# Both scans of a tile couple first, then both products with C, on VectorE

## The chip, the cores and the metric

The kernel runs on one core of one Trainium2 chip. The metric is the device time of one execution in microseconds; a comparison is made between runs of the two kernels on the same chip. In the text, DVE is VectorE, ACT is ScalarE, POOL is GpSimd, PE is TensorE and SP is SyncE, whose queue issues all the transfers spoken of here.

## The reference

The reference is a small network of four layers on an image batch of 4 x 96 x 64 x 64 in float32. Layer 0 is a selective scan (a state-space block) over four directions of each image; layer 1 is an inverted-residual convolution; layer 2 a Fourier mixing layer with a quantised feed-forward; layer 3 linear attention with another quantised feed-forward. The change is in layer 0. Cut to its core, with 192 channels `d`, 16 states `n` and 4 directions `k`, each of 4096 positions:

```python
def step(hst, inp):                       # one position
    ut, dt_, bt, ct = inp
    dA = jnp.exp(dt_[..., None] * A[None])
    hst = hst * dA + (dt_ * ut)[..., None] * bt[:, :, None, :]
    y = jnp.einsum('bkdn,bkn->bkd', hst, ct)
    return (hst, y)
_, ys = jax.lax.scan(step, h0, (u_t, d_t, B_t, C_t))
```

So for each channel and state there is a first-order recurrence along the positions, and the output sums, over the 16 states, the state times `C`.

## The kernel before

**Tiles.** One step of the scan stage handles one image, one direction and one chunk of 512 positions; there are 4 x 4 x 8 = 128 steps. The 192 x 16 recurrences of a step lie in 12 units. A unit, here called a couple, has two tiles of 128 partitions x 512 positions, e = 0 and e = 1. The functions that make a couple are nested in `scans`:

- `inputs` (L1213): POOL multiplies `rep_g` (delta times u) by B into the buffer `db`, both tiles in one instruction (L1215). There are 3 `db` buffers.
- `decays` (L1217): ACT computes exp(delta times A) into two of the four PSUM banks with the tag `da`, one instruction for each e (L1225). Just before each of the two it calls `keep` for the couple two places back.
- `states` (L1227): DVE runs the recurrence as a tensor-tensor scan over `da` and `db` (L1234). Of the 12 couples of a step, 5 (`POOL_C`) have the scan's result written into the buffer `hc` in SBUF, and POOL multiplies it by C afterwards, both tiles in one instruction (`product`, L1253). In the other 7 the scan writes in place, into its `da` bank, and DVE itself multiplies by C into `hc` (L1238). There are 5 `hc` buffers.
- `keep` (L1240): the last column of the scanned tile is copied to `state`, where the next chunk of the same direction starts. ACT does it for each e (L1248) where DVE made the product, POOL for both at once (L1250) where POOL makes it.
- `sums` (L1263): PE adds up the 16 states of two couples with the constant `stack` matrix, into the bank `y` (L1274), first for the later couple and there for e = 1. After the last couple of a pass, ACT copies `y` to `yt` (L1285).

An exponential may overwrite a `da` bank only when the couple that used it has been scanned and, where DVE makes the product, multiplied and kept.

**Order.** The scan stage is recorded under a manual schedule: every engine executes its instructions in the order in which Python emits them. The loop over slots emits, for the couple `units[slot]`:

```python
decays(units[slot + 1], units[slot - 1] if slot > 0 else None)
...
product(units[slot - 1])
...
inputs(units[slot + 2])
...
states(x)
for group in due.get(slot, ()):
    sums(group)
```

`product` is called only for a couple whose product POOL makes. After these calls, the loop calls `advance` as long as the slot has room: it emits single instructions of the other layers' work, here called side work, by a planner with estimated costs (`WORK`, `RATE`, `SHARE`). So the side work of PE, ACT and DVE stands between one couple and the next, at places that don't depend on the measured time. The loads of `rep_d`, `rep_g` and `rep_BC`, 512 KB each, are issued by SP at fixed couples of a step (`LOADS`).

**Waits.** Instructions of different engines, and dependent instructions of one engine, are held together by semaphores. `keep` on ACT waits for DVE's product of the same e, the second exponential of a slot for whatever used its bank.

Of the kernel before, what the change touches and what calls it, by code (L numbers as in the profile page):

```python
# [94 lines left out]
def hybrid_kernel(ctx: ExitStack, tc: tile.TileContext, a: dict):  # L95
# [10 lines left out]
    pool = lambda name, bufs=1, **kw: ctx.enter_context(tc.tile_pool(name=name, bufs=bufs, **kw))  # L106
# [75 lines left out]
    def pair(tag):  # L182
        return sp.tile([128, 2, CH], F32, name=tag, tag=tag, bufs=SCAN[tag])
# [973 lines left out]
    def scans(stages):  # L1157
# [69 lines left out]
        def states(x):  # L1227
            step, u = x["step"], x["u"]
            order = slice(None, None, -1) if step["k"] >= 2 else slice(None)
            x["hc"] = pair("hc")  # L1230
            x["h"] = [x["hc"][:, e] for e in (0, 1)] if x["pool"] else x["da"]
            for e in (0, 1):
                start = 0.0 if step["n"] == 0 else steps[x["number"] - 1]["last"][:, 2 * u + e : 2 * u + e + 1]
                nc.vector.tensor_tensor_scan(  # L1234
                    x["h"][e][:, order], x["da"][e][:, order], x["db"][:, e, order], start, ALU.mult, ALU.add
                )
                if not x["pool"]:
                    x["made"] = nc.vector.tensor_mul(x["hc"][:, e], x["h"][e], x["step"]["BC"][x["j"]][:, 1])  # L1238

        def keep(x, e):  # L1240
# [61 lines left out]
        for slot in range(len(units) + 6):  # L1302
            clock[0] = slot
            x = units[slot] if slot < len(units) else None
# [23 lines left out]
            if x is not None:  # L1328
                states(x)
# [252 lines left out]
```

## Time and profile before

| What | us |
|---|---|
| median of 3 runs | 6582.01 |
| lowest and highest run | 6569.84, 6595.57 |
| profiled execution, first to last instruction | 6603.1 |
| of that, from the first scan (79.2) to the end of the last (6129.9) | 6050.7 |
| after it | 473.2 |
| scans in place, 1792, busy and mean | 2278.6, 1279 ns (with a state), 1219 ns (without) |
| scans into `hc`, 1280, busy and mean | 1557.3, 1266 ns (with a state), 1203 ns (without) |
| DVE's products with C, 1792, busy and mean | 1239.3, 692 ns |
| POOL's `db`, 1536, busy and mean | 3601.2, 2365 ns |
| POOL's products with C, 640, busy and mean | 1512.0, 2363 ns |
| ACT's exponentials, 3072, busy and mean | 2067.3, 690 ns |

The profiled execution's own time is shown only as this span, from its first instruction to its last. It is one execution, and the runs are others; the counts are of instructions. Busy time is what the profiler records of an instruction from its start to its end; neighbours on one engine may overlap a little, so starts tell more than durations. The profile also tells how long an engine sat idle ahead of an instruction and which instruction of another engine ended that wait.

### The profile page before, as it was taken

What the parts mean: (1) busy time and instruction counts of PE and PEld (TensorE: products, weight loads), DVE (VectorE), ACT (ScalarE), POOL (GpSimd) and SP (SyncE); (2) the same over time, 40 slices, a digit from 0 to 9 for tenths busy, and PEclk for the clock granted to TensorE, in tenths of its full rate; (3) what the DMA queues carried; (4) which work ended last, traced back from release to release, by engine and by line L of the source; (5) the groups of instructions that cost most, each with busy time, mean ns of one, the idle gap of its engine ahead of it and who ended that gap; (6) DMA issues with size and microseconds to landing.
All of it is one profiled execution on the core that took longest, in us unless ns stands there. A gap on an engine that the chain in (4) does not pass through costs nothing. (4 is left out here: it accounts for less than half of the span.)

```text
span 6603.1 us, 84466 instructions
## 1 busy us (share of the span) xinstructions
PE 4803.7 (73%) x27804; PEld 1767.2 (27%) x27804; DVE 5616.6 (85%) x5947; ACT 4265.1 (65%) x8152; POOL 5183.5 (79%) x2743
## 2 busy tenths in 40 slices
PE   7633857757987776775688877667887776758997
PEld 2100212111224521221122254211223621112383
DVE  5979999999999889999899998988999889898113
ACT  5743777765665677787466657766665677756356
POOL 4757878789998889987899988988999788898100
PEclk9755978868998877886799878878988877979998
DMA  5644565676544544466764455465644544655131
GB/s 186 200 153 136 188 202 188 198 234 226 178 155 158 178 151 144 161 196 195 239 211 159 148 175 172 140 225 176 188 155 154 176 153 165 198 191 170 34 97 40
DMA packets 438826, 1121.42 MB, mean 170 GB/s; under 512 B 73002, under 2 KB 74768, under 8 KB 437140
## 3 DMA queue, kind: packets, MB, share of 16 engines
q1 hardware_dynamic: 438388, 1116.02, 51.6%
q8 instruction: 221, 3.62, 0.2%
q14 instruction: 217, 1.78, 0.1%
HBM read 881.28 MB, written 239.01 MB: 170 GB/s over the span
## 5 line engine op out<-in xcount | busy, mean ns | idle before, releaser
L1215 POOL TENSOR_TENSOR db<-rep_g,rep_BC 128x1024 f32<-128x1024 f32 x1536 | 3601.2, 2365 | 474.3 <-DVE ps_da L1234 357.7
L1225 ACT ACTIVATE ps_da<-rep_d,aneg 128x512 f32<-128x512 f32 x3072 | 2067.3, 690 | 557.2 <-DVE hc L1234 423.1
L1234 DVE TENSOR_TENSOR_SCAN ps_da<-ps_da,state,db 128x512 f32<-128x512 f32 x1568 | 2005.6, 1279 | 209.8 <-ACT state L1248 162.0
L1253 POOL TENSOR_TENSOR hc<-hc,rep_BC 128x1024 f32<-128x1024 f32 x640 | 1512.0, 2363 | 116.0 <-DVE hc L1234 59.4
L1274 PE MATMUL ps_y<-hc,cst 128*32 128x512 f32 x6144 | 1024.8, 745 | 660.9 <-POOL hc L1253 413.4
L1234 DVE TENSOR_TENSOR_SCAN hc<-ps_da,state,db 128x512 f32<-128x512 f32 x1120 | 1371.3, 1266 | 82.2 <-ACT ps_da L1225 54.8
L1238 DVE TENSOR_TENSOR hc<-ps_da,rep_BC 128x512 f32<-128x512 f32 x1792 | 1239.3, 692 | 109.8 <-PE ps_y L1274 1.5
L1248 ACT COPY state<-ps_da 128x1 f32<-128x1 f32 x1568 | 247.8, 158 | 525.4 <-DVE hc L1238 521.5
L1274 PEld LDWEIGHTS ps_y<-hc,cst 128*32 128x32 f32 x6144 | 145.9, 118 | 1298.1 <-POOL hc L1253 641.4
L1250 POOL COPY state<-hc 128x2 f32<-128x2 f32 x560 | 106.8, 191 | 353.1 <-DVE hc L1234 337.1
L805 PE MATMUL ps_mm<-h,wd 128*32 128x512 f32 x3192 | 366.9, 595 | 8.7 <-ACT r L154 8.7
L543 PE MATMUL ps_mm<-xp,taps 128*128 128x512 f32 x576 | 299.5, 663 | 52.2 <-ACT ua L545 21.5
L1234 DVE TENSOR_TENSOR_SCAN ps_da<-ps_da,db 128x512 f32<-128x512 f32 x224 | 273.0, 1219 | 41.0 <-ACT state L1248 27.8
L782 PE MATMUL ps_mm<-wd,w 128*32 128x512 f32 x2128 | 272.0, 621 | 37.7 <-DMA wd<-x 22.3
L1285 ACT COPY yt<-ps_y 128x512 f32<-128x512 f32 x256 | 149.1, 582 | 162.8 <-PE ps_y L1274 161.2
L594 PE MATMUL ps_mm<-xd,dtw 128*128 128x512 f32 x256 | 171.0, 760 | 101.3 <-ACT z L616 56.2
L955 PE MATMUL ps_mm<-wa,xp 128*64 128x96 f32 x1728 | 139.7, 324 | 88.8 <-DVE d L959 71.5
L864 PE MATMUL ps_mm<-r,cst 128*128 128x512 f32 x208 | 146.6, 794 | 70.7 <-ACT r L861 17.8
L1234 DVE TENSOR_TENSOR_SCAN hc<-ps_da,db 128x512 f32<-128x512 f32 x160 | 186.0, 1203 | 3.0 <-ACT ps_da L1225 2.9
L786 ACT ACTIVATE h<-ps_mm 128x512 f32<-128x512 f32 x266 | 152.4, 596 | 48.2 <-PE ps_mm L782 46.6
L543 PEld LDWEIGHTS ps_mm<-xp,taps 128*128 128x128 f32 x576 | 116.7, 210 | 230.4 <-issue 163.2
L805 PEld LDWEIGHTS ps_mm<-h,wd 128*32 128x32 f32 x3192 | 105.5, 109 | 251.9 <-issue 210.1
(405 smaller groups left out, 6856.2 us busy)
## 6 DMA issues: line engine op xcount, KB each, us to landing
rep_BC<-bc SPq DMA_DIRECT2D x512, 512.0 KB
rep_g<-du SPq DMA_DIRECT2D x384, 512.0 KB
rep_d<-delta SPq DMA_DIRECT2D x384, 512.0 KB
y<-yt SPq DMA_DIRECT2D x512, 128.0 KB
du<-g SPq DMA_DIRECT2D x128, 256.0 KB
delta<-z SPq DMA_DIRECT2D x128, 256.0 KB
tab<-in_etab SPq DMA_DIRECT2D x128, 256.0 KB
ypart<-y SPq DMA_DIRECT2D x72, 256.0 KB
```

The lines of the kernel that those rows point to most:

```text
L543: mm(p, lhsT=taps[:, t, 0:128], rhs=window(t, c + e), start=t == 0, stop=t == 8)
L594: mm(p, lhsT=dtw[:, o + 2 * part, 0:128], rhs=xd, start=True, stop=True)
L782: mm(p[32 * n : 32 * n + 32], lhsT=w1[:, 32 * g : 32 * g + 32], rhs=xin[:, n : n + 15 : 2, 1 : W + 1], start=True, stop=True)
L786: act(h[:, :, 1 : W + 1], split(p), AF.Relu)
L805: mm(p[32 * n : 32 * n + 32], lhsT=held["wd"][:, groups[i], o, dx, :], rhs=here[i][:, :, dx : dx + W], start=dx == 0, stop=dx == 2)
L1215: nc.gpsimd.tensor_mul(x["db"], x["step"]["g"][x["i"]], both(x["step"]["BC"][x["j"]][:, 0]))
L1225: act(x["da"][e], x["step"]["d"][x["i"]][:, e], AF.Exp, scale=aneg[:, av : av + 1])
L1234: nc.vector.tensor_tensor_scan(x["h"][e][:, order], x["da"][e][:, order], x["db"][:, e, order], start, ALU.mult, ALU.add)
L1238: x["made"] = nc.vector.tensor_mul(x["hc"][:, e], x["h"][e], x["step"]["BC"][x["j"]][:, 1])
L1248: nc.scalar.copy(to[:, e : e + 1], x["h"][e][:, end : end + 1])
L1253: x["made"] = nc.gpsimd.tensor_mul(x["hc"], x["hc"], both(x["step"]["BC"][x["j"]][:, 1]))
L1274: done = mm(y[32 * q : 32 * q + 32], lhsT=const("stack"), rhs=x["hc"][:, e], start=first or (x["pass"] == 0 and x["j"] == 0), stop=last or ...
```

## The change

In `states`, the product with C leaves the loop over e that issues the scans and gets a loop of its own behind it. In the 7 couples of a step whose product DVE makes, DVE's order becomes scan 0, scan 1, product 0, product 1, where it was scan 0, product 0, scan 1, product 1. The other 5 couples keep their order. The product's line becomes L1239, and the lines behind it move by one.

```diff
             for e in (0, 1):
                 start = 0.0 if step["n"] == 0 else steps[x["number"] - 1]["last"][:, 2 * u + e : 2 * u + e + 1]
                 nc.vector.tensor_tensor_scan(
                     x["h"][e][:, order], x["da"][e][:, order], x["db"][:, e, order], start, ALU.mult, ALU.add
                 )
-                if not x["pool"]:
+            if not x["pool"]:
+                for e in (0, 1):
                     x["made"] = nc.vector.tensor_mul(x["hc"][:, e], x["h"][e], x["step"]["BC"][x["j"]][:, 1])
```

## The prediction

> **What bounds the kernel now.** I read the busy shares first, then the slices, then three stretches, then single VectorE (DVE) instructions, then the waits.
>
> The page's busy shares and two of its rows of slices:
>
> ```profile
> PE 4803.7 (73%) x27804; PEld 1767.2 (27%) x27804; DVE 5616.6 (85%) x5947; ACT 4265.1 (65%) x8152; POOL 5183.5 (79%) x2743
> ...
> DVE  5979999999999889999899998988999889898113
> ...
> POOL 4757878789998889987899988988999788898100
> ```
>
> DVE leads, but GpSimd (POOL) is close, and both stop after slice 37: the scan stage runs from 79 to 6130 us, and a tail of 473 us follows it that the change doesn't touch. The scan stage has 128 steps of 12 couples; cutting it at every 24th scan shows three kinds of step. One of each, from the view by stretches (length, then each engine's busy time and instruction count):
>
> ```profile
> 1276.03:1329.75 53.72, 35.83 (x94) 6.98 (x87) 52.63 (x58) 43.03 (x85) 41.57 (x23) 0.82 0.61 196
> 3575.69:3616.28 40.59, 32.09 (x174) 10.24 (x166) 39.14 (x45) 25.25 (x52) 40.19 (x23) 0.92 0.50 165
> 4022.60:4069.22 46.62, 39.31 (x326) 25.73 (x325) 38.60 (x39) 33.30 (x59) 41.37 (x24) 0.82 0.61 195
> ```
>
> The columns are PE, weight loads, DVE, ACT, POOL. The first step is DVE's alone (52.6 of 53.7). In the second POOL is busy for 40.2 of 40.6 and DVE for 39.1: both are full. In the third nobody is full; DVE waits there for ACT. I sorted all 128: **DVE-full**, 30 steps, 1475 us, DVE 47.7 us busy a step; **both full**, 36 steps, 1486 us, mean 41.3 us with POOL 39.8 and DVE 40.1; **waiting**, 62 steps, 3090 us, with 418 us of DVE waits over 0.1 us.
>
> Where DVE's time goes inside a couple, from the timeline of DVE alone (start, duration; "x2" is two in a row):
>
> ```profile
> 1276.03 1.28 DVE L1234 TENSOR_TENSOR_SCAN ps_da<-ps_da,state,db 128x512 f32<-128x512 f32 x1
> 1277.35 0.69 DVE L1238 TENSOR_TENSOR hc<-ps_da,rep_BC 128x512 f32<-128x512 f32 x1
> 1277.95 1.28 DVE L1234 TENSOR_TENSOR_SCAN ps_da<-ps_da,state,db 128x512 f32<-128x512 f32 x1
> 1279.27 0.69 DVE L1238 TENSOR_TENSOR hc<-ps_da,rep_BC 128x512 f32<-128x512 f32 x1
> 1279.88 2.45 DVE L1234 TENSOR_TENSOR_SCAN hc<-ps_da,state,db 128x512 f32<-128x512 f32 x2
> 1282.24 0.67 DVE L609 SCALAR_TENSOR_TENSOR ps_mm<-ps_mm,z 128x512 f32<-128x512 f32 x1
> ```
>
> Read starts, not durations. A product that reads the scan just before it starts 1.32 us after that scan: the scan's whole 1.28 plus 0.04. An instruction that doesn't depend on its predecessor starts before that one is recorded as ended: scan 2 comes 0.60 after product 1, whose record is 0.69 long, and the two scans of the last couple, whose product POOL makes, take 2.36 together, so 1.18 each. Over the trace the medians are: first scan to product 1358 ns, second scan to product 1316, product to anything 608, scan to independent scan 1190, scan to anything else independent 1175. So each scan-to-product step pays some 0.14 us for the dependence.
>
> Who waits for whom, in three lines of the waits:
>
> ```profile
> DVE ps_da L1234 <- ACT state L1248: 189.9, 97, 7.5
> POOL db L1215 <- DVE ps_da L1234: 357.7, 167, 42.6
> ACT state L1248 <- DVE hc L1238: 521.5, 405, 45.7
> ```
>
> DVE waits for ACT in 97 places, POOL hardly ever holds DVE up, and ACT and POOL wait for DVE more than it waits for them.
>
> [...] and POOL's `db` product has a median of 2362 ns over 1536 of them, so I expect no effect from the new order on POOL's durations.
>
> **The change, part by part.** Nothing is added or removed. In the 896 couples whose product DVE makes (1792 products, L1238), scan 2 moves ahead of product 1. The built programs show POOL's and SP's instructions in the same order with the same waits, so no transfer moves; PE's and ACT's order is the same too, and only some waits shift to a neighbouring instruction.
>
> *DVE.* Before: 1.32 + 0.61 + 1.32 + 0.61 = 3.86 us for a couple (3.85 in the lines above, 3.89 from the medians). After: scan 1 to scan 2 1.19, scan 2 to product 1 1.18, then 0.61 + 0.61 = 3.59. Product 2 needs scan 2, whose end at 1.19 + 1.28 + 0.04 = 2.51 lies before its turn at 2.98. Two in-place scans in a row don't occur before; the lower bound is 1.18 (scans into `hc`), the upper 1.32 (a full dependence). I take 1.19[...]. The gain is 0.27 to 0.31, I take 0.29: 896 x 0.29 = 260 us of DVE time. That is the ceiling.
>
> *ACT.* `keep` e = 0 and the exponential behind it wait for product 1, which now ends 3.06 us after the couple's start instead of 2.01. Behind them in ACT's queue stand `keep` e = 1 and the second exponential, waiting for product 2 in either order, and then the side work, so nothing else is held up. Product 2 ends at 3.67 instead of 3.94. ACT still has the first exponential (0.69) to do then, so the second starts 0.35 after product 2, not 0.23: 3.67 + 0.35 = 4.02 against 4.17, 0.15 earlier. What the first exponential fills is scanned at least one couple (2.36) later. Cost: nothing, while that cover holds.
>
> *POOL and PE.* Scan 2 frees `db` at 2.47 instead of 3.21, so POOL may start sooner; PE's sums wait for product 2, 0.27 sooner. No cost.
>
> *What of the 260 lies on the path.* I followed the trace from the last scan to the first, at each instruction to whichever came last, the engine's own predecessor or a wait. 921 of the 1792 products are on that chain: 336 in DVE-full steps, 280 in both-full ones, 305 in waiting ones. At 0.145 each these are 49, 41 and 44 us. In DVE-full steps POOL (39.5 busy of 49 us) leaves room: I take 47. In both-full steps POOL is next: its intervals (2.32 for each of 12 `db`, 2.58 for each of 5 products with its copy) make 40.7 of the mean 41.3: I take 15. In waiting steps a DVE that comes sooner partly waits longer for ACT, which sits behind matmuls: I take 33. Sum 95 us. The span of 6603.1 us would become 6508, a factor of 0.9856. The profile shows no time around that span; it lay 21 us above the median of the runs, and I apply the factor to the median: 6582 x 0.9856 = 6487 us.
>
> **Rivals.**
>
> *Full conversion (faster still).* If ACT's waits are themselves set by DVE (it waited 521.5 us for products), waiting steps gain the full 7 x 0.29 = 2.0 us. 92 steps outside "both full" x 2.0 = 184, plus 22: about 205 us, 6378 us. Against it: the chain holds only 305 products in those 62 steps, and it runs mostly through PE there.
>
> *No overlap, or hidden (no change).* If in-place scans in PSUM follow each other only at 1.28 to 1.32, the couple takes 3.78 to 3.86; with half on the chain, 0 to 40 us. Or POOL, PE and ACT together take up all but the DVE-full steps, and half of those: 25 us. About 6557 us. For it: three engines near full in the second stretch.
>
> *The second exponential comes late (slower).* Scan 2 is now due 1.19 after scan 1, not 1.93. In the changed program 239 DVE couples take for scan 2 a bank that scan 2 of the couple just before, a POOL one, has just left. There the exponential can start 2.49 after that couple's start and ends at 3.18, visible at about 3.25; scan 2 is due at 2.36 + 1.19 = 3.55. The slack falls from 1.0 to 0.3 us. If ACT is late by x there, DVE loses x - 0.3 in each: the gain of 95 is gone from x = 0.7, and slower by 0.5% from 0.84. With one 0.69 exponential and a 0.58 copy ahead, x = 1.27 costs 232 us: net 137 slower, 6719 us. Against it: ACT is busy for 65% and mostly waits for DVE.
>
> **How the numbers follow.** Forecast 0.60, full conversion 0.17, no change 0.16, slower 0.07. The likeliest gives 6487 us. Its own range is a gain of 55 to 140. For 8 in 10 it reaches up into full conversion (185 us: 6397) and down to a gain of 15 us (6567). A measurement of this kernel can tell about 0.5%, 33 us, from no change: faster needs a gain over 33, which the forecast and full conversion hold nearly whole; slower by as much takes the third rival.
>
> **What would show it.** In the changed profile, two scans in a row and then two products should start 1.19, 1.18 and 0.61 apart, and the couple take 3.58 to 3.62; the mean idle time ahead of the products (L1239 then) should fall from 61 ns to about nothing. DVE-full steps should lose about 2 us each, both-full ones stay at 40.5 to 41, POOL's share of the scan stage rise from 85% to 87%. DVE's waits for ACT should grow from 293 us by some 100. Scans 1.28 or more apart prove the no-change rival; DVE waits for ACT that grow by more than 260 us, ahead of second scans, prove the slower one; a shift of ACT's side work that leaves the waits as they are proves full conversion.

## The result and the profile after

| What | before | after |
|---|---|---|
| median of the runs, us | 6588.79 | 6488.82 |
| lowest and highest run | 6569.84, 6598.30 | 6478.26, 6495.32 |
| ratio after/before, 95% interval | | 0.9848 [0.9828, 0.9867] |
| profiled execution, span, us | 6603.1 | 6476.4 |
| of that, scan stage | 6050.7 | 5924.4 |
| after the scan stage | 473.2 | 473.7 |

The change saves 100 us, 1.5%. The forecast was 6487 us, the factor 0.9856. The two profiled executions lie 127 us apart, more than the medians: the one of before took some 15 us longer than its median run, the one of after some 10 us less (its run took 6478.26 us, 1.9 us more than its span). So differences between the two profiles are read below for where the time went, and the runs for how much.

First the busy shares of the changed kernel:

```profile
PE 4756.9 (73%) x27804; PEld 1748.4 (27%) x27804; DVE 5432.5 (84%) x5947; ACT 4244.3 (66%) x8152; POOL 5175.7 (80%) x2743
```

The same instructions, the same counts, but DVE is busy for 184 us less. Nothing was left out, so its records got shorter or overlap more. The timeline of DVE alone shows how. It is a later couple of the step whose first couples the prediction shows, step 22, which now begins 26 us earlier (start, duration, "x2" is two in a row):

```profile
1257.57 2.46 DVE L1234 TENSOR_TENSOR_SCAN ps_da<-ps_da,state,db 128x512 f32<-128x512 f32 x2
1259.93 1.27 DVE L1239 TENSOR_TENSOR hc<-ps_da,rep_BC 128x512 f32<-128x512 f32 x2
1261.12 0.69 DVE L609 SCALAR_TENSOR_TENSOR ps_mm<-ps_mm,z 128x512 f32<-128x512 f32 x1
```

The couple starts at 1257.57 and the next instruction, one of the side work, at 1261.12: 3.55 us, where it took 3.85 in the lines of before. Two in-place scans from start to start of the first product take 2.36, just like two scans into `hc`. Over the whole trace the medians are: scan to scan 1191 ns, scan 2 to product 1 1175, product 1 to product 2 591, product 2 to the next instruction 594; the couple 3551, before 3903.

The groups of instructions give the sum (busy time, mean ns, idle time ahead and what ended most of it). Before:

```profile
L1234 DVE TENSOR_TENSOR_SCAN ps_da<-ps_da,state,db 128x512 f32<-128x512 f32 x1568 | 2005.6, 1279 | 209.8 <-ACT state L1248 162.0
L1238 DVE TENSOR_TENSOR hc<-ps_da,rep_BC 128x512 f32<-128x512 f32 x1792 | 1239.3, 692 | 109.8 <-PE ps_y L1274 1.5
```

and after:

```profile
L1234 DVE TENSOR_TENSOR_SCAN ps_da<-ps_da,state,db 128x512 f32<-128x512 f32 x1568 | 1923.9, 1272 | 314.8 <-ACT state L1249 209.9
L1239 DVE TENSOR_TENSOR hc<-ps_da,rep_BC 128x512 f32<-128x512 f32 x1792 | 1134.9, 674 | 0.1
```

The idle time ahead of the products, 109.8 us before (61 ns for each), is 0.1. Their busy time is 104 us less, with a mean of 674 ns instead of 692. A second scan now overlaps the first in the records, and the first group's busy time is 82 us less. Against that, the in-place scans wait longer than they did.

Three steps, the same ones as shown of before (steps 22, 72 and 82), and a fourth, step 100, that is needed later, from the view by stretches (length; busy time and count of PE, weight loads, DVE, ACT, POOL; the clock granted to PE as a share of full speed, the DMA engines' busy share, GB/s):

```profile
1249.58:1301.62 52.04, 36.93 (x96) 7.69 (x94) 51.08 (x57) 42.71 (x84) 41.44 (x23) 0.74 0.64 206
3505.64:3546.60 40.96, 33.90 (x190) 9.62 (x182) 37.89 (x45) 26.36 (x54) 40.56 (x23) 0.92 0.48 168
3936.57:3976.83 40.26, 32.95 (x326) 21.32 (x323) 37.05 (x40) 32.61 (x59) 39.05 (x22) 0.92 0.66 208
...
4748.01:4788.58 40.57, 31.46 (x224) 7.94 (x228) 38.79 (x43) 29.09 (x59) 40.17 (x23) 0.87 0.50 164
```

Step 22, DVE's own, is 1.7 us shorter and still DVE's. In step 72 POOL is now busy for 40.56 of 40.96 us and DVE for 37.89: DVE works 1.3 us less, and the step is no shorter. Step 82 lost 6 us, but not to the change: its granted clock was 0.82 before and is 0.92 here, and in a second profile of the changed kernel (run again below, beside "More couples to POOL"), where it is 0.81, the step takes 45.66 us. Single waiting steps move that much between executions. Sums over the kinds are steadier:

| Kind, steps | us before | after | for each step | DVE busy in a step |
|---|---|---|---|---|
| DVE-full, 30 | 1474.6 | 1421.3 | -1.78 | 47.7 to 45.9 |
| both full, 36 | 1485.8 | 1465.7 | -0.56 | 40.1 to 38.8 |
| waiting, 62 | 3090.0 | 3037.0 | -0.85 | 42.4 to 41.0 |

The granted clock differs between the two executions as a whole too, 0.828 and 0.839. The gain doesn't hang on it: in the second profile of the changed kernel the DVE-full steps have a mean clock of 0.763, as before, and take 1424 us against 1475.

Last the idle time of DVE ahead of its scans, from the view of one line's instructions. Before:

```profile
  ACT state L1248: 199.5, 106
  ACT ps_da L1225: 102.9, 57
  POOL db L1215: 17.6, 16
  PE ps_y L1274: 13.9, 2
  issue: 0.3, 1
```

and after:

```profile
  ACT state L1249: 240.4, 122
  ACT ps_da L1225: 84.2, 49
  POOL db L1215: 79.4, 68
  issue: 47.0, 42
...
```

ACT together went from 302 to 325 us. What grew is POOL's `db`, by 62 us, and "issue", time for which the profile shows no releaser, by 47. All these waits lie ahead of first scans; ahead of second scans there is none of over 60 ns.

### The profile page after: what moved, and what is told of

The parts are those of the page before. It is cut to its first block, busy times and chain, and to the rows that moved or that the text cites. A ratio compares the mean times of both kernels' runs of the same rounds, so it can differ in the third digit from the quotient of the medians.

```text
span 6476.4 us, 84592 instructions
## 1 busy us (share of the span) xinstructions
PE 4756.9 (73%) x27804; PEld 1748.4 (27%) x27804; DVE 5432.5 (84%) x5947; ACT 4244.3 (66%) x8152; POOL 5175.7 (80%) x2743
## 3 DMA queue, kind: packets, MB, share of 16 engines
q8 instruction: 221, 3.62, 0.2%
## 5 line engine op out<-in xcount | busy, mean ns | idle before, releaser
L1215 POOL TENSOR_TENSOR db<-rep_g,rep_BC 128x1024 f32<-128x1024 f32 x1536 | 3597.3, 2364 | 344.3 <-DVE ps_da L1234 232.3
L1234 DVE TENSOR_TENSOR_SCAN ps_da<-ps_da,state,db 128x512 f32<-128x512 f32 x1568 | 1923.9, 1272 | 314.8 <-ACT state L1249 209.9
L1275 PE MATMUL ps_y<-hc,cst 128*32 128x512 f32 x6144 | 1009.2, 735 | 626.4 <-POOL hc L1254 366.7
L1239 DVE TENSOR_TENSOR hc<-ps_da,rep_BC 128x512 f32<-128x512 f32 x1792 | 1134.9, 674 | 0.1
L609 DVE SCALAR_TENSOR_TENSOR ps_mm<-ps_mm,z 128x512 f32<-128x512 f32 x192 | 131.7, 686 | 58.3 <-ACT z L607 55.0
```

The source lines that it names most:

```text
L1215: nc.gpsimd.tensor_mul(x["db"], x["step"]["g"][x["i"]], both(x["step"]["BC"][x["j"]][:, 0]))
L1234: nc.vector.tensor_tensor_scan(x["h"][e][:, order], x["da"][e][:, order], x["db"][:, e, order], start, ALU.mult, ALU.add)
L1275: done = mm(y[32 * q : 32 * q + 32], lhsT=const("stack"), rhs=x["hc"][:, e], start=first or (x["pass"] == 0 and x["j"] == 0), stop=last or ...
```

## The experiments

Each ratio is to the kernel before, on the same chip, with its 95% interval. Diffs are against the changed kernel unless said otherwise.

**One dependence back.** The products in the order 1, 0: product 1 stands directly behind the scan that it reads, everything else of the change stays.

```diff
             if not x["pool"]:
-                for e in (0, 1):
+                for e in (1, 0):
```

> The couple's order is scan 0, scan 1, product 1, product 0: scan 2 stays early and frees the db buffer early, but the first of the two products now reads the scan just ahead of it. Theory (the dependence behind a scan is what the change took away): one of the two dependences is back, so scan 1 to product 1 takes 1.32 us instead of 1.18, the couple some 3.70 us, between 3.55 (changed kernel) and 3.89 (before). Of the change's gain of 1.5% about 0.85% is left: ratio to before 0.990 to 0.993. Rival (scan 2 and db earlier are the gain): nothing is given back, ratio 0.985. Rival (ACT's first exponential must not be later): product 0 ends 0.6 us later still, so ACT's waits grow and the ratio goes to 1.0 or above.

Measured: 6544.41 us, 0.9929 [0.9916, 0.9941], 44 us under its before (6587.95). The theory's range held. Its timeline of DVE:

```profile
1265.28 2.46 DVE L1234 TENSOR_TENSOR_SCAN ps_da<-ps_da,state,db 128x512 f32<-128x512 f32 x2
1267.78 1.29 DVE L1239 TENSOR_TENSOR hc<-ps_da,rep_BC 128x512 f32<-128x512 f32 x2
1268.98 2.45 DVE L1234 TENSOR_TENSOR_SCAN hc<-ps_da,state,db 128x512 f32<-128x512 f32 x2
```

The two scans still follow each other (2.46 together), but the first product now comes 2.50 after the couple's start, not 2.36, and the couple takes 3.70, its median over the trace 3753 ns. By the medians the couple keeps 0.15 of its 0.35 us, and the run 44 of its 100 us; the dependence put back costs the rest. The second scan stands as early here as in the changed kernel, and `db` is free as early, so neither saves these 56 us. ACT's copies wait longer than in the changed kernel, 669 us for products instead of 493, but DVE waits less for ACT ahead of its scans (275 us against 325), so the loss doesn't come by way of ACT either. It is shown that this part of the gain comes from the distance between a scan and the product that reads it. That the other 44 us have the same cause is argued from the proportion: 0.15 of 0.35 us for a couple, 44 of 100 us for the run.

**Only some of the steps.** `LATE` lists the steps that have the new order; the others keep the old one. Once these are the 30 DVE-full steps, once the 62 waiting ones.

```diff
+LATE = (3, 4, 5, 7, 12, ...)
...
+                if not x["pool"] and x["number"] not in LATE:
+                    x["made"] = nc.vector.tensor_mul(...)
-            if not x["pool"]:
+            if not x["pool"] and x["number"] in LATE:
```

> The new order only in the 30 steps that were DVE-full in the profile before; the other 98 keep the old one. Theory (each step gains for itself): the steps named lost 53 us together between the two profiles, so the ratio to before is 0.992 (6536 of 6589 us), and the other steps stay as they were. Rival (the gain is carried from step to step, or is spread evenly over the 128 steps): 30 of 128 of 100 us, 23 us, ratio 0.9965.

> The new order only in the 62 waiting steps. Theory: these lost 53 us between the two profiles, ratio 0.992. Rival (in waiting steps ACT and PE set the pace, and what the profiles show there is chance between two executions): below 20 us, ratio above 0.997. With the run on the DVE-full steps the two gains add up to the whole change less what the both-full steps gave (20 us of 126).

Measured: DVE-full alone 6538.18 us, 0.9922 [0.9909, 0.9936], 50 us; waiting alone 6551.71 us, 0.9940 [0.9927, 0.9954], 36 us. The first is what the theory said, the second lies between the two answers: the waiting steps gain clearly, but less than the 0.992 named there, which the 53 us of the profile would give. In the trace of the first, the waiting steps, which it leaves alone, are 23 us shorter than in the profiled execution of before, and the both-full ones 2 us longer; so some 20 of those 53 us belong to that one execution of before and not to the change (the granted clock of these steps was 0.812 there, and 0.825 in this trace). The 36 us of the runs are the better figure. If the parts add up, the 100 us leave 14 for the 36 both-full steps. The profiles agree: these steps took 1486 to 1488 us in the three kernels that keep the old order in them, and 1466 and 1470 in the two profiles of the changed kernel, 16 to 22 us less.

**POOL relieved, before and after.** Both kernels without POOL's product with C in couples 3 and 10 of a step, so without 256 of its 640 products.

```diff
-                nc.vector.tensor_tensor_scan(
+                x["scan"] = nc.vector.tensor_tensor_scan(
...
         def product(x):
+            if x["u"] in (3, 10):
+                x["made"] = x["scan"]
+                return
             x["made"] = nc.gpsimd.tensor_mul(...)
```

> The kernel before, leaving out POOL's product with C in couples 3 and 10 of each step (their states go to PE unmultiplied); all else as before. POOL loses 2 x 2.32 = 4.6 us a step. Theory (before the change DVE and POOL are both full in 36 steps): those become DVE's alone and lose only 41.3 - 40.4 = 0.9 us each, 32 us; DVE-full steps nothing; waiting ones in which POOL sets the pace some 20 us. Ratio to before 0.992. Rival (POOL already sets the pace alone): 36 x 4 and more, 0.97.

> The changed kernel, leaving out the same two POOL products in each step. Theory (in both-full steps POOL took up what DVE gave): with POOL out of the way the change brings its 7 x 0.34 = 2.4 us in each of the 36 both-full steps too, less what ACT and PE hold, so some 2.0; against the cut kernel with the old order that is 72 + 55 + 60 = about 190 us, and the ratio to before 0.963 to 0.967. Rival (PE, or the latency between engines, holds those steps): the change brings no more than the 100 us it brings uncut, 0.976 to 0.978.

Measured: before with the cut 6567.57 us, 0.9969 [0.9958, 0.9979]; after with the cut 6430.51 us, 0.9763 [0.9749, 0.9777]. Both gained less than the theory said, and the second fell on the rival's figure. But the pair is worth more than either: with POOL relieved the change brings 137 us (6430.51 to 6567.57), without it 100. Step 100, both full, shows why. Here it is before, then in the kernel before with the cut, and then in the changed one with the cut:

```profile
4852.98:4893.98 41.00, 32.76 (x228) 8.34 (x232) 40.20 (x44) 28.83 (x60) 40.26 (x23) 0.83 0.47 164
```

```profile
4832.18:4873.18 41.00, 30.96 (x224) 7.95 (x224) 40.20 (x43) 28.95 (x60) 35.58 (x20) 0.88 0.48 163
```

```profile
4713.26:4752.61 39.35, 30.62 (x220) 7.67 (x220) 38.69 (x44) 28.77 (x59) 35.69 (x21) 0.87 0.50 175
```

In the kernel before, 4.7 us less of POOL changed nothing, 41.00 and 41.00: DVE held the step, however full POOL was. After the change the same cut brings 1.2 us (40.57 to 39.35). Over all 36 both-full steps the cut brought 3 us before and 33 after, and the change itself 20 us uncut and 50 with the cut. So DVE was the bound of these steps before, POOL is now, and POOL keeps about 30 us of what the change gives there. The cut also spares PE's sums their wait for the two products, so alone it doesn't tell POOL's time from that wait; the next experiment leaves POOL's work as it is.

**Still less DVE.** The changed kernel, with the scan of e = 1 writing into `hc` and DVE's product of e = 1 left out.

```diff
-            x["h"] = [x["hc"][:, e] for e in (0, 1)] if x["pool"] else x["da"]
+            x["h"] = [x["hc"][:, e] for e in (0, 1)] if x["pool"] else [x["da"][0], x["hc"][:, 1]]
...
-                for e in (0, 1):
+                for e in (0,):
```

> The changed kernel, leaving out DVE's product of tile e = 1 in each of the 896 couples: its scan writes into hc, and the states go to PE unmultiplied. DVE loses 896 x 0.59 = 530 us more. Theory (after the change POOL, and ACT with PE, set the pace outside the DVE-full steps): both-full steps 0 to -0.5 us each, DVE-full ones -3.5 (down to POOL's 41), waiting ones a third of 4.1, in all some 200 us, 40% of what DVE gives; ratio to before 0.953 to 0.958. Rival (DVE alone bounds the scan stage): 400 us or more, 0.925.

Measured: 6369.78 us, 0.9671 [0.9657, 0.9684], short of both figures. The 896 products took 0.59 us of DVE each, 530 us, and 119 us of run time came out, 22%. By kind: both-full steps 1465.3 us, after 1465.7, so nothing at all, though DVE's busy time there fell from 38.8 to 35.0 us a step; DVE-full 66 us less than after, waiting 38 less. The waits of DVE say what held it instead:

```profile
DVE ps_da L1234 <- POOL db L1215: 200.3, 121, 10.2
...
DVE hc L1234 <- POOL db L1215: 99.6, 92, 6.5
```

300 us for `db`, where the changed kernel has 79 and the one before 18; of the 300, 140 are in the both-full steps. So it is POOL's work that makes the 40.7 us of a both-full step.

**POOL's copies of the last column to ACT.** In 37 steps in which POOL is nearly full, ACT makes the `keep` copies of POOL's couples.

```diff
                 if not x["pool"]:
                     nc.scalar.copy(...)
+                elif x["number"] in KEEP_ACT:
+                    nc.scalar.copy(to[:, e : e + 1], x["h"][e][:, end : end + 1])
                 elif e == 0:
                     nc.gpsimd.tensor_copy(to, x["hc"][:, :, end])
```

> The changed kernel, and in 37 steps in which POOL is busy for over 95% of the step after the change, ACT makes the copy of the last column for the couples that POOL multiplies too (two copies of 128 x 1, 0.16 us each, in place of one POOL copy of 0.19). Theory (POOL took up what DVE gave in both-full steps): POOL loses 5 x 0.27 = 1.3 us a step, DVE needs 38.5 of the 40.8 us, so a step gets 0.7 to 1.3 us shorter, 26 to 48 us in all: ratio to before 0.978 to 0.981, below the changed kernel's 0.985. Rival (PE, or the latency between engines, holds these steps): nothing, 0.985. Rival (the POOL product now waits for ACT): longer, 0.987 or more.

Measured: 6519.05 us, 0.9898 [0.9884, 0.9912], 30 us worse than the changed kernel. The rival was right. POOL multiplies `hc` in place, so its product waits for the copy; the waits of POOL have a line that the changed kernel lacks:

```profile
POOL hc L1257 <- ACT state L1252: 81.6, 56, 4.5
```

The 37 steps took 32 us more than in the changed kernel, the other 91 together 0.2 us more; against the second profile of the changed kernel the 37 took 20 us more. Here, handing an instruction of 0.2 us to an engine that comes to it late cost more than it freed.

**More couples to POOL.** POOL multiplies 6 or 7 couples, not 5, in some steps in which DVE is the bound; DVE makes one or two pairs of products fewer there. First in 21 steps, then in the 17 of them that count as DVE-full, with the changed kernel beside it.

```diff
-                                      "pool": u in POOL_C})
+                                      "pool": u in on_pool})
```

Here `on_pool` is (1, 3, 5, 7, 9, 11) or (1, 3, 5, 6, 8, 10, 11) in the listed steps, and `POOL_C` in all others.

> The changed kernel, and in DVE-heavy steps POOL multiplies more couples by C: 6 of 12 in ten steps, 7 of 12 in eleven, where it was 5. Each moved couple takes 3.55 - 2.37 = 1.18 us from DVE and adds 2.58 us to POOL. Theory (these steps are DVE's alone): 10 x 1.18 + 11 x 2.36 = 38 us, ratio to before 0.979, below the changed kernel's 0.985. Rival (two POOL products so close together hold up PE's sums or the hc buffers): 0.985 or more.

> The changed kernel as it is, again, on the same chip as the next kernel, so that the two can be compared within one call. Both theories: 0.984 to 0.986 of the kernel before, as measured.

> The changed kernel, but POOL multiplies 6 of the 12 couples in eight, and 7 of 12 in nine, of the 30 steps in which DVE was full, and 5 as ever in all others. DVE loses 25 pairs of products, each some 1.2 us, 30 us in all. In the kernel with 21 such steps those of the 30 lost 78 us by profile against 53 in the changed kernel. If DVE still bounds those steps: 25 us less than the changed kernel of this call, a ratio of 0.980 to 0.982. Rival: the path moves to POOL or ACT as soon as DVE is relieved, so that at most a third of the 30 us shows: 0.983 to 0.986, not to be told from the changed kernel.

Measured: in 21 steps 6473.70 us, 0.9829 [0.9815, 0.9843]; in 17 steps 6471.28 us, 0.9827 [0.9814, 0.9841]; the changed kernel itself 6487.72 us, 0.9849 [0.9836, 0.9863]. The first fell between its two answers: by the ratios it brings some 13 of the 38 us. On the chip where both ran, the 17 steps bring 16 us, half of the 30 us taken off DVE, between the two answers; the five runs reach from 6467.09 to 6482.30 us, those of the changed kernel from 6481.66 to 6495.89. The ratios' intervals still overlap a little, so the 16 us are likely rather than certain. By profile the 30 DVE-full steps took 26 us less than in the changed kernel beside it; the waiting ones took 6 us more. The two kernels with more couples on POOL are the fastest of those that leave nothing out, the second 116 us under before.

## Why the prediction was right, point by point

**The total.** 95 us were forecast, 100 came out (99.7 where the changed kernel ran again). By kind the forecast said 47, 15 and 33 us; the two kernels with a part of the change measured 50 for the DVE-full and 36 for the waiting steps, which leaves 14. The split was right too, as far as the runs tell: the ratios' intervals leave some 9 us open on each of the two parts measured, and more on the 14, which is a difference of three figures.

**The couple: mis-sized, 0.34 to 0.35 against 0.29 us.** The scan-to-scan step (1.19 taken, 1191 ns measured) and scan 2 to product 1 (1.18, 1175) were right. Two terms were too small. The old scan-to-product steps went into the sum as 1.32 each from the lines shown, but the medians, 1358 and 1316, make 1337: 308 ns saved for a couple instead of 270. The 0.29 was taken between the two, and the "some 0.14 us" for a dependence is the smaller of two values: the prediction's own medians give 183 ns behind the first scan and 141 behind the second. And the products were put in unchanged at 0.61. They take 591 and 594 ns now, 31 ns less for the two; in the kernel before, all but two of DVE's products stand behind their own scan. So the couple came out at 3.55 us, under the 3.58 to 3.62 that were named as the sign. The ceiling is then 896 x 0.34 = 305 us, not 260.

**What of it lies on the path.** 95 of 260 was forecast, 37%; 100 of 305 came, 33%. So the larger couple gain didn't carry through in proportion; the two deviations nearly cancel, and the closeness of the total owes something to that.

**DVE-full steps.** Forecast "about 2 us each": 1.78 by profile, 1.68 in the second profile of the changed kernel, 1.7 by the runs (50 us in 30 steps).

**Both-full steps.** Forecast 40.5 to 41 with POOL next at 40.7: they take 40.7 (40.8 in the second profile), and they stay at 40.7 when DVE loses another 3.8 us a step. POOL's share of the scan stage rose to 87%, as forecast. DVE's waits in these steps grew from 10 to 66 us, those for `db` from 1 to 25 and those for ACT ahead of scans from 8 to 26. This step of the prediction is the best supported of all.

**Waiting steps: the amount right, the waiter wrong.** I expected DVE's waits for ACT to grow by some 100 us. Over the whole scan stage those ahead of scans grew by 22, and in the 62 waiting steps they fell, from 277 to 265 us (256 in the second profile). What grew in these steps is the wait for `db`, from 16 to 50 us, and idle time with no releaser shown, from none to 40. The failed step is "a DVE that comes sooner partly waits longer for ACT"; that 36 us came where 33 were forecast is luck in part. With POOL's cut the waits for `db` in these steps are no shorter (54 us), so they don't come from the two products left out there. What bounds the waiting steps now isn't settled: with POOL's cut they lost 27 us more than without, and 31 us in the kernel before, of which some 20 are that profile's own. A kernel that relieves ACT or PE in these steps alone wasn't tried.

**ACT, POOL and PE at no cost.** Two lines of the changed kernel, from its groups (ACT's `keep`, busy, mean, idle time ahead) and from its waits (us, times, longest):

```profile
L1249 ACT COPY state<-ps_da 128x1 f32<-128x1 f32 x1568 | 246.9, 157 | 502.9 <-DVE hc L1239 493.4
```

```profile
POOL db L1215 <- DVE ps_da L1234: 232.3, 112, 43.5
```

ACT's copies waited 493 us for the products, before 522, so ACT waited no longer for a product that comes later in the couple. POOL's `db` waited 232 us for scans instead of 358, as the earlier release of `db` should give. The mean of `db` stayed at 2364 ns (2365), so the new order didn't disturb POOL; that it wouldn't was an estimate of mine, which no trace had shown beforehand. PE's sums waited 166 us for DVE's products instead of 238.

**The rivals.** *Full conversion* (205 us): refuted by the runs; even 530 us less of DVE's work brought only 119. The sign named for it, waits for ACT that stay as they are, nearly came true without it (302 and 325 us), so it was a weak sign. *No overlap, or hidden*: scans follow each other at 1.19, and the DVE-full and the waiting steps gained 50 and 36 us, where this rival left 25 us in all; what is true of it is that POOL keeps some 30 us in the both-full steps. *The second exponential comes late*: no second scan waits, where 239 couples were at stake. That ACT's work moved forward together with DVE's, because about half of ACT's waits in the scan stage are for DVE (1070 of 2002 us before, 917 of 1898 after), fits this, but no run tests it.

## What to carry to other kernels

Where an engine issues a result and its reader back to back, read the time between starts, not the durations: here the dependence cost 0.15 us each, and another independent instruction between the two took it away without any work added. Before such a saving is multiplied by its count, sort the program's stretches by what bounds them: of 305 us a third came through, half of it in the quarter of the steps that this engine bounded alone. An engine that was nearly as full as the bound (POOL 39.8 us of a both-full step before, DVE 40.1) became the bound here, and a cut of that second engine, in the kernel before and in the one after, showed which of the two holds a stretch, where the busy shares couldn't.

## What was not expected of the hardware

- A product with C takes 591 to 594 ns to the next start with a record of 674 when it stands behind another instruction than its own scan, and 608 with a record of 692 behind its own scan (608 and then 598, with a mean record of 686, where only the first product of the couple stands so). So the step behind a dependent product is longer too, by 17 and 14 ns (608 against 591 and 594). Why the record is longer isn't shown.
- The dependence costs 183 ns after the first scan (1358 against 1175; over all 894 such steps of the trace before the median is 1368) and 141 after the second (1316 against 1175). Where only one is left, after the second scan and with no product between the scans, it is 1357, so it isn't the scan's place e that sets it. It goes with the product's place: a couple's first product starts 90 to 104 ns after the recorded end of its scan, in the kernel before (median 91) and in the one with one dependence back, and the second one of before 35 ns after it. Why is open.
- A scan takes 1175 ns from start to start where a product of the same size takes 591, a ratio of 1.99 (medians of the trace after, 896 steps each). Why isn't shown.
- In step 100 two engines were busy for 98% of the time, and cutting one of them by 12% changed the step's length by nothing (41.00 us both times). Busy for 98% didn't mean bound here.
